# An attention and FP4 network block on one core: v's product in four column groups, row sums on GpSimd, the shift through DRAM, and a later network

## The chip, the cores and the metric

The kernel runs on one core of one Trainium2 chip. A time is device microseconds of one execution of the whole program. Three runs of the kernel before took 4761.64, 4766.83 and 4768.15 us; the median is 4766.83 us. A core has five engines with an instruction stream each: TensorE (PE, with its weight loads shown apart as PEld), VectorE (DVE), ScalarE (ACT), GpSimd (POOL) and SyncE (SP), which issues all DMAs of this program. Each engine executes its stream in order; semaphores tie the streams together.

## The reference

The input x has 8 batches of 1024 tokens with 512 features, in float32. Cut to what matters:

```python
xn = layernorm(x)                                  # no scale, no bias
q, k, v = split(xn @ W_attn + b_attn, 3)           # 16 heads of 32 features
att = softmax(where(causal, q @ k.T * 32**-0.5, -inf))
attn = (att @ v) @ W_proj + b_proj
fq = fp4_quant_dequant                             # blocks of 16: scale = max|x| / 6, round to E2M1
h = silu(fq(xn) @ fq(w_gate).T) * (fq(xn) @ fq(w_up).T)      # 1408 hidden features
out = x + attn + fq(h) @ fq(w_down).T
```

## The kernel before, in words

Tokens are worked on in 64 tiles of 128. Attention is worked on in 64 units, each two heads (HU) of one batch; a batch has eight tiles and eight units.

`prepare` takes a normalised tile, transposes it, keeps its quantised form for the network in DRAM (`keep_quantised`), and at every second tile calls `project`, which makes q, k and v for two tiles in six steps. q and k are split into a rounded part and a rest, `high` and `low`, so that the scores can be made with one-pass float32r products; they go to DRAM with v. In the kernel before v carries a 33rd column of ones per head (VW = 33), so that the product of weights and v yields the row sums too.

`maxima(un)` makes all scores of a unit once (L407), masks the diagonal blocks and takes row maxima on VectorE (L415, L417). The negated maxima, again in a rounded part and a rest, are placed in a sparse tile `shift`, transposed in four pieces (L433) and copied to `shT` by ScalarE (L435).

`weigh(un)` makes the scores a second time, keys along partitions. For each half Q of the queries and each block j of 128 keys, and for each head r, one product adds the shift (L466), another the scores (L469), ScalarE takes the exponential (L477) into a buffer `pr` (eight of them), and GpSimd clears what lies above the diagonal (L480). The products with v are delayed: `weighted()` issues those of the waiting key blocks (L449, fp32, heads at partitions 0 and 64 of one PSUM tile `y`) after the scores of a later block. In the kernel before this is called at every odd j and at the end, so the blocks hold keys 0, then 1 and 2, then 3 and 4, and so on. The result is copied by ScalarE (L498) and stored; `invert` fetches the row sums of a unit, takes reciprocals on VectorE and stores them.

`network` goes through the tiles in chunks of 512, 512 and 384 hidden features: gate and up products (L557), SiLU on ScalarE, product and quantisation on VectorE (`quantised`, ten instructions), transposes (L215), and the down product (L542). Its result plus x and the projection's bias is kept in DRAM as `part`. `finish` fetches y and the inverses of a tile, multiplies them (L625), multiplies with W_proj (L632; its two halves come again and again through a ring with one buffer), adds `part` (L637) and stores the output.

What sets the order. TensorE, ScalarE and SyncE follow the order in which the Python program emits instructions; VectorE and GpSimd are ordered by a scheduler from the dependencies. `merge` interleaves several generators ("streams"): each yields the estimated cost of what it has just emitted, and the next to go on is the one that has got least far through the total given for it. `Later(us, action)` emits an action, mostly a DMA, when the sum of all yielded costs has grown by so much. The loop over n runs, for unit n, these streams together: `begin(n + AHEAD)` (the preparation of a tile ten units ahead), `finish` of an earlier tile, `weigh(units[n])`, one tile of the network, and `maxima(units[n + 1])`. The network lags by LAG = 5 units: in units 0 to 4 the remaining pieces of the network's weights are quantised instead, and the first eight tiles are quantised (`prepare_late`). There are 34 weight pieces, of which a third is quantised ahead of the loop, in the head, where the first batch is projected. After the loop follow the last tiles of the network and the remaining calls of `finish`.

PSUM has six buffers named g that all products share in turn, one buffer y and one buffer acc.

## Time and profile before

| | value |
|---|---|
| median of three runs | 4766.83 us |
| the profiled execution: its own time / its span | 4757.63 us / 4755.9 us |
| granted clock of TensorE over the span | 0.976 of full speed |
| TensorE / VectorE / ScalarE / GpSimd busy | 4490.6 / 2794.9 / 1505.3 / 491.1 us |
| DMA | 590.38 MB, queue busy 44.7% of 16 engines |
| y (L449), 3072 records | 606.8 us busy |
| exponentials (L477), 1536 | 668.7 us busy |
| selects (L480), 1024 | 360.0 us busy |
| first / last record of L449 | 209.8 us / 4555.1 us |

How to read it. The span is that of the profiled execution, from its first to its last instruction. Busy time of a group is the time in which at least one of its instructions ran, so overlapping instructions count once; the mean is that of one. An fp32 product appears as two records with a weight load each, a float32r product as one. "Idle before" is the time in which the engine stood still ahead of the group, and the arrow names what ended the wait. In the chain of work that ended last each step is followed back to what released it.

### The profile page before, as it was taken

What the parts mean: (1) busy time and instruction counts of PE and PEld (TensorE: products, weight loads), DVE (VectorE), ACT (ScalarE), POOL (GpSimd) and SP (SyncE); (2) the same over time, 40 slices, a digit from 0 to 9 for tenths busy, and PEclk for the clock granted to TensorE, in tenths of its full rate; (3) what the DMA queues carried; (4) which work ended last, traced back from release to release, by engine and by line L of the source; (5) the groups of instructions that cost most, each with busy time, mean ns of one, the idle gap of its engine ahead of it and who ended that gap; (6) DMA issues with size and microseconds to landing.
All of it is one profiled execution on the core that took longest, in us unless ns stands there. A gap on an engine that the chain in (4) does not pass through costs nothing.

```text
span 4755.9 us, 54933 instructions
## 1 busy us (share of the span) xinstructions
PE 4490.6 (94%) x17876; PEld 2693.5 (57%) x17876; DVE 2794.9 (59%) x6841; ACT 1505.3 (32%) x2906; POOL 491.1 (10%) x1177
## 2 busy tenths in 40 slices
PE   7677899999999999999999999999999999999995
PEld 6445555555555555655555656556556555555553
DVE  6698466655556565656655656555656654566542
ACT  2133333333333333333333333333333333333310
POOL 0011111110110110110110011010111110111100
PEclk9888999999999999999999999999999999999997
DMA  6644434444453453544454454443454444333233
GB/s 208 181 138 137 111 102 109 132 128 130 114 150 106 123 135 107 139 132 117 125 146 118 121 146 118 123 128 115 128 145 122 132 123 127 98 98 94 65 91 108
DMA packets 582590, 590.38 MB, mean 124 GB/s; under 512 B 131616, under 2 KB 445984, under 8 KB 582304
## 3 DMA queue, kind: packets, MB, share of 16 engines
q1 hardware_dynamic: 582304, 586.88, 44.7%
q8 instruction: 142, 2.33, 0.2%
q14 instruction: 144, 1.18, 0.1%
HBM read 434.12 MB, written 152.57 MB: 123 GB/s over the span
## 4 chain that ended last, share of the span: by engine, by line
PE 83%; DVE 7%; DMA 6%; issue 1%; ACT 1%; SPq 1%; POOL 0%; DVEq 0%; ACTq 0%; POOLq 0%
PE g L557 24%; PE acc L542 11%; PE y L449 10%; PE g L315 8%; PE g L407 6%; PE g L466 5%; PE g L469 5%; PE g L632 5%; PE g L352 4%; PE g L215 2%; DMA inv_y<-inv_kept 2%; DVE scale L195 1%; DMA wp<-in_L_attn_W_proj_dram 1%; DMA qs<-qk_kept 1%; PE g L433 1%
## 5 line engine op out<-in xcount | busy, mean ns | idle before, releaser
L477 ACT ACTIVATE pr<-g 128x512 f32<-128x512 f32 (+3 forms) x1536 | 668.7, 492 | 1082.0 <-PE g L469 1072.8
L417 DVE TENSOR_REDUCE neg<-g 128x1 f32<-128x512 f32 (+3 forms) x1024 | 585.3, 582 | 230.0 <-PE g L407 225.7
L466 PE MATMUL g<-shT,pick 128*128 128x512 f32 (+3 forms) x1536 | 672.2, 447 | 20.3 <-DVE neg L417 16.3
L557 PE MATMUL g<-wgT,xqT_in 128*128 128x512 f32 (+1 forms) x1536 | 674.9, 566 | 13.8 <-DMA xqT_in<-xq_kept 13.4
L407 PE MATMUL g<-ks,qs 128*128 128x512 f32 (+3 forms) x1536 | 664.0, 477 | 18.5 <-DVE neg L417 11.4
L542 PE MATMUL acc<-wdT,hqT 128*128 128x512 f32 x1408 | 672.2, 599 | 1.4 <-ACT hqT L216 1.4
L480 POOL TENSOR_SCALAR_AFFINE_SELECT pr<-pr 128x128 f32<-128x128 f32 x1024 | 360.0, 366 | 3021.8 <-ACT pr L477 3005.5
L557 PE MATMUL g<-wuT,xqT_in 128*128 128x512 f32 (+1 forms) x1536 | 671.5, 562 | 0.0
L449 PE MATMUL y<-pr,vs 128*33 128x512 f32 (+3 forms) x3072 | 606.8, 497 | 2.9 <-POOL pr L480 2.7
L415 DVE TENSOR_TENSOR g<-g,mask 128x128 f32<-128x128 f32 x1024 | 289.3, 293 | 482.4 <-PE g L407 477.1
L469 PE MATMUL g<-qs,ks 128*128 128x512 f32 (+3 forms) x1536 | 516.9, 348 | 0.0
L315 PE MATMUL g<-xnT,wa 128*128 128x256 f32 x2048 | 486.9, 393 | 29.4 <-DVE scale L196 12.9
L315 PEld LDWEIGHTS g<-xnT,wa 128*128 128x128 f32 x2048 | 398.4, 198 | 108.2 <-ACT xnT L216 13.9
L407 PEld LDWEIGHTS g<-ks,qs 128*128 128x128 f32 x1536 | 280.4, 191 | 306.1 <-issue 139.8
L557 PEld LDWEIGHTS g<-wgT,xqT_in 128*128 128x128 f32 x1536 | 278.5, 191 | 237.5 <-issue 184.1
L557 PEld LDWEIGHTS g<-wuT,xqT_in 128*128 128x128 f32 x1536 | 276.0, 189 | 216.4 <-issue 167.8
L542 PEld LDWEIGHTS acc<-wdT,hqT 128*128 128x128 f32 x1408 | 255.7, 189 | 230.4 <-issue 215.0
L466 PEld LDWEIGHTS g<-shT,pick 128*128 128x128 f32 x1536 | 293.6, 191 | 154.4 <-issue 65.7
L469 PEld LDWEIGHTS g<-qs,ks 128*128 128x128 f32 x1536 | 293.8, 191 | 96.8 <-issue 64.6
L449 PEld LDWEIGHTS y<-pr,vs 128*33 128x33 f32 x3072 | 138.9, 110 | 354.5 <-issue 278.2
L572 DVE TENSOR_TENSOR hid<-hid,g 128x512 f32<-128x512 f32 (+1 forms) x192 | 122.7, 639 | 306.8 <-PE g L557 288.7
L632 PE MATMUL g<-wp,yT 128*128 128x256 f32 x1024 | 253.3, 392 | 47.5 <-DVE yT L625 27.9
(87 smaller groups left out, 4201.2 us busy)
## 6 DMA issues: line engine op xcount, KB each, us to landing
wa<-in_L_attn_W_attn_dram SPq DMA_DIRECT2D x194, 512.0 KB
wp<-in_L_attn_W_proj_dram SPq DMA_DIRECT2D x131, 512.0 KB
qs<-qk_kept SPq DMA_DIRECT2D x512, 128.0 KB
ks<-qk_kept SPq DMA_DIRECT2D x512, 128.0 KB
qk_kept<-high SPq DMA_DIRECT2D x128, 256.0 KB
qk_kept<-low SPq DMA_DIRECT2D x128, 256.0 KB
res<-in_L_attn_x_dram SPq DMA_DIRECT2D x72, 256.0 KB
v_kept<-v SPq DMA_DIRECT2D x64, 264.0 KB
```

Of the source, the lines that this page charges most:

```text
L315: nc.tensor.matmul(pq[:, j, :], lhsT=wa[:, c, j * P : (j + 1) * P], rhs=xnT[:, c, :], start=(c == 0), stop=(c == NC - 1),)
L407: nc.tensor.matmul(sc[:, :n], lhsT=un.qs[Q][:, r, i * P : (i + 1) * P], rhs=un.ks[h][:, r, :n], start=True, stop=True,)
L415: nc.vector.tensor_tensor(sc[:, n - P : n], sc[:, n - P : n], mask, ALU.add)
L417: nc.vector.tensor_reduce(dst, sc[:, :n], AX.X, ALU.max, negate=True)
L449: nc.tensor.matmul(y[r * 2 * HD : r * 2 * HD + VW, q0:], lhsT=un.vs[h][:, jj, r, :], rhs=pr[:, q0:], start=(j == 0), stop=(j == last), ski ...
L466: nc.tensor.matmul(w[:, q0:], lhsT=pick[:, Q * HU + r, :], rhs=un.shT[:, q0:], start=True, stop=False)
L469: nc.tensor.matmul(w[:, q0:], lhsT=un.ks[h][:, r, jj * P : (jj + 1) * P], rhs=un.qs[Q][:, r, q0:], start=False, stop=True,)
L477: nc.scalar.activation(pr[:, q0:], w[:, q0:], AF.Exp)
L480: nc.gpsimd.affine_select(out=pr[:, q0 : q0 + P], in_=pr[:, q0 : q0 + P], compare_op=ALU.is_ge, fill=0.0, base=0, pattern=[[1, P]], channe ...
L542: nc.tensor.matmul(tl.acc, lhsT=job.hqT[:, j, :], rhs=wdT[:, i, :], start=(i == 0), stop=(i == NI - 1))
L557: nc.tensor.matmul(job.g[:, : job.w], lhsT=job.tl.xqT[:, c, :], rhs=wT[:, c, job.i0 : job.i0 + job.w], start=(c == 0), stop=(c == NC - 1),)
L632: nc.tensor.matmul(po[:, cols], lhsT=yT[:, c, :], rhs=wp[:, c, :], start=(c == 0), stop=(c == NC - 1))
```

## The change

The change has several parts.

- v loses its column of ones. Its product is placed in four groups of 32 columns: even and odd key blocks of the two heads each have 32 partitions of `y`. The blocks now hold keys 0 and 1, 2 and 3, and so on, issued after the scores of the next even block; block 1 of Q = 0 is widened by cleared columns so that both of the first two start the accumulation at full width. `y` is stored in two halves, which `finish` adds.
- The row sums come from GpSimd: `summed` adds the exponentials of a head over all key blocks into `sum0` and `sum1`, and at the end of each Q four fp32 products with a tile of ones (128 x 32) add up the partitions into `z`, 256 columns each, in the four column groups. A new `yield 0.8` stands ahead of the last block.
- The shift's 32 rows (high and rest, two Q, two heads, four tiles) are put side by side, transposed in one piece, copied, stored in DRAM and fetched with four DMAs into one of two constant `shT` tiles.
- LAG is 8 in place of 5, DRAM buffers are 4 in place of 3, half of the weight pieces are done in the head in place of a third, and the two wide products with a spread scale in each weight piece are on GpSimd.
- `low` is written over `full`, and v is copied into a buffer of `full`'s name, in place of buffers of their own. `step` has one buffer in place of two.
- `finish` comes ten units after its tile in place of nine, fetches `part` ahead of the product, adds in two halves, and for the last units uses a resident W_proj in the buffers that the ring of W_attn no longer needs. After the loop, one `finish` stands beside each network tile.
- `up_to` carries what it ran over its budget to the next call. Stream totals: weigh 18 in place of 19, maxima 7 in place of 6.5, `begin` of an even n 4 in place of 1.

```diff
-    LAG = 5
+    LAG = 8
...
+    ones = const.tile([P, HD], F32, name="ones")
+    nc.gpsimd.memset(ones, 1.0)
...
     for k in range(2):
-        sh = const.tile([P, QG, P], F32, name=f"shift{k}")
-        nc.gpsimd.memset(sh, 0.0)
+        sh = const.tile([P, W], F32R, name=f"shT{k}")
+        nc.vector.tensor_copy(sh, zeros)
         shifts.append(sh)
-    v_out = const.tile([P, QT, HEADS // 2, VW], F32, name="v")
...
+        spreader = spreader or nc.vector
+        spreader.tensor_tensor(blocks(xs), blocks(src), spread(inv), ALU.mult)
...
+        spreader.tensor_tensor(blocks(xs), blocks(xs), spread(scale), ALU.mult)
...
-            done.append((piece, quantised(raw, piece[4], raw)))
+            done.append((piece, quantised(raw, piece[4], raw, nc.gpsimd)))
...
-                low = p1.tile([P, 2, QW], F32R, name="low")
+                low = full.bitcast(F32R)
...
+            v_out = p1.tile([P, QT, 2 * P], F32, name="full")
+            nc.scalar.copy(v_out, pv)
...
-        for i in range(QG):
-            nc.tensor.transpose(pt[:, i * P : (i + 1) * P], sh[:, i, :], ident)
-        un.shT = p2.tile([P, W], F32R, name="shT")
-        nc.scalar.copy(un.shT, pt)
-        yield 0.5
+        nc.tensor.transpose(pt[:rows, :P], stat.rearrange("p e q r i -> p (e q r i)"), ident)
+        statT = p2.tile([rows, P], F32, name="statT")
+        nc.scalar.copy(statT, pt[:rows, :P])
+        yield 0.3
+        def store():
+            un.shift = dram.tile([2, 2, HU, W], F32, name="shift_kept")
+            nc.sync.dma_start(out=un.shift.rearrange("e q r (i p) -> (e q r i) p", p=P), in_=statT)
+            Later(2.5, load)
+        def load():
+            un.shT = shifts[un.n % 2]
+            for q in range(2):
+                for r in range(HU):
+                    row = (q * HU + r) * HD
+                    nc.sync.dma_start(out=un.shT.bitcast(F32)[row : row + 2, :], in_=un.shift[:, q, r, :])
+        Later(2.0, store)
...
+            sums = [p1.tile([P, W], F32, name=f"sum{r}") for r in range(HU)]
+            def summed(group):
+                for r in range(HU):
+                    prs = [(pr, q0) for _, s, pr, q0 in group if s == r]
+                    if group[0][0] == 0:
+                        nc.gpsimd.tensor_tensor(sums[r], prs[0][0], prs[1][0], ALU.add)
+                    else:
+                        for pr, q0 in prs:
+                            nc.gpsimd.tensor_tensor(sums[r][:, q0:], sums[r][:, q0:], pr[:, q0:], ALU.add)
...
+                    row = (j % 2 * HU + r) * HD
                     nc.tensor.matmul(
-                        y[r * 2 * HD : r * 2 * HD + VW, q0:],
-                        lhsT=un.vs[h][:, jj, r, :],
+                        y[row : row + HD, q0:],
+                        lhsT=un.vs[h][:, jj, r * HD : (r + 1) * HD],
                         rhs=pr[:, q0:],
-                        start=(j == 0),
-                        stop=(j == last),
+                        start=(j < 2),
+                        stop=(j >= last - 1),
                         skip_group_check=True,
+                        tile_position=(0, row),
                     )
...
-                if j % 2 == 1 and waiting:
+                if j % 2 == 0 and waiting:
                     yield weighted()
                     waiting = []
                 waiting += fresh
-            yield weighted()
+                if j % 2 == 1:
+                    summed(waiting)
+            yield 0.8
+            spent = weighted()
+            z = ps_g.tile([P, W // 2], F32, name="g")
+            for r in range(HU):
+                for half in range(2):
+                    row = (r * 2 + half) * HD
+                    nc.tensor.matmul(
+                        z[row : row + HD, :],
+                        lhsT=ones,
+                        rhs=sums[r][:, half * W // 2 : (half + 1) * W // 2],
...
+                        tile_position=(0, row),
+                    )
+            yield spent + 0.45
...
-        EARLY = PIECES // 3
+        EARLY = PIECES // 2
...
-            if n >= NT + 1:
-                streams.append((finish(tiles[n - NT - 1]), 6.4))
-            streams.append((weigh(units[n]), 19.0))
+            if n >= LAG + 2:
+                streams.append((finish(tiles[n - LAG - 2]), 6.4))
+            streams.append((weigh(units[n]), 18.0))
...
-        left = [finish(tiles[n]) for n in range(N - NT - 1, N)]
-        for n in range(N - LAG, N):
-            count = 1 if n in (N - LAG, N - 1) else 2
-            some, left = left[:count], left[count:]
-            merge([(up_to(net, TILE), TILE), (itertools.chain(*some), 6.4 * count)])
-        next(left[0])
+        for n in range(N, N + LAG):
+            some = [finish(tiles[m]) for m in ([n - LAG - 2] if n == N else []) + [n - LAG - 1]]
+            merge([(up_to(net, TILE), TILE), (itertools.chain(*some), 6.4 * len(some))])
+        end = finish(tiles[N - 1])
+        passed(next(end))
         run(net)
-        for step in left:
-            run(step)
+        run(end)
```

## The prediction

> **What bounds the kernel now.** First the page's busy shares and its 40 slices, then the chain that ended last, then the trace in five stretches, and last the groups, the timeline and the waits around the lines that change.
>
> ```profile
> PE 4490.6 (94%) x17876; PEld 2693.5 (57%) x17876; DVE 2794.9 (59%) x6841; ACT 1505.3 (32%) x2906; POOL 491.1 (10%) x1177
> PE   7677899999999999999999999999999999999995
> PE g L557 24%; PE acc L542 11%; PE y L449 10%; PE g L315 8%; PE g L407 6%; PE g L466 5%; PE g L469 5%; PE g L632 5%; PE g L352 4%; PE g L215 2%; DMA inv_y<-inv_kept 2%; DVE scale L195 1%; DMA wp<-in_L_attn_W_proj_dram 1%; DMA qs<-qk_kept 1%; PE g L433 1%
> ```
>
> TensorE is full except in the first five slices and the last. Its work is spread over many lines, and L449, the product with v, is 10% of the chain. GpSimd has 90% free. The stretches are: head, units 0 to 4 without the network, units 5 to 53, units 54 to 63 (no projections left), tail. The columns are length, then busy time of TensorE, weight loads, VectorE, ScalarE, GpSimd, then clock, DMA share and GB/s.
>
> ```profile
> 0.00:209.80 209.80, 150.16 (x636) 122.60 (x638) 125.22 (x303) 38.38 (x80) 11.10 (x31) 0.89 0.68 204
> 209.80:514.10 304.30, 218.29 (x1003) 141.87 (x1002) 252.25 (x663) 97.07 (x210) 44.72 (x97) 0.84 0.48 132
> 514.10:3985.00 3470.90, 3409.40 (x13649) 2040.50 (x13648) 2030.12 (x4968) 1157.71 (x2220) 366.82 (x880) 0.99 0.46 125
> 3985.00:4555.20 570.20, 567.86 (x2175) 306.88 (x2176) 321.95 (x779) 198.21 (x373) 64.47 (x167) 1.00 0.34 90
> 4555.20:4755.90 200.70, 144.92 (x424) 81.61 (x424) 65.32 (x133) 13.90 (x24) 4.03 (x3) 0.88 0.35 105
> ```
>
> In the third and fourth stretches (4041 us) TensorE is idle for only 64 us: there a microsecond of TensorE work removed is a microsecond gained, 70.8 us a unit in the third (3470.9 / 49), 57.0 in the fourth. Units 0 to 4 take 61 us each without any network, with VectorE busy 83%: quantising weights and late tiles sets their pace. The tail idles 56 us.
>
> ```profile
> L449 PE MATMUL y<-pr,vs 128*33 128x512 f32 (+3 forms) x3072 | 606.8, 497 | 2.9 <-POOL pr L480 2.7
> L433 PE MATMUL g<-ident,shift 128*128 128x128 f32 x256 | 39.0, 275 | 5.4 <-DVE rstd L260 2.3 <-DVE inv L198 2.2 <-DVE shift L427 0.7
> L539 POOL TENSOR_TENSOR res<-res,bp 128x512 f32<-128x512 f32 x64 | 85.0, 1328 | 597.4 <-DMA res<-in_L_attn_x_dram 467.4 <-DVE hid L207 37.6 <-DVE hid L572 33.8
> L480 POOL TENSOR_SCALAR_AFFINE_SELECT pr<-pr 128x128 f32<-128x128 f32 x1024 | 360.0, 366 | 3021.8 <-ACT pr L477 3005.5 <-DMA res<-in_L_attn_x_dram 7.3 <-POOL pr L480 0.3
> ```
>
> The timeline at one block of four y products (8 records of 512 columns), with its neighbours:
>
> ```profile
> 2542.43 0.59 PE L632 MATMUL g<-wp,yT 128*128 128x256 f32 x2
> 2542.96 1.91 PE L449 MATMUL y<-pr,vs 128*33 128x512 f32 x8
> 2544.80 0.44 PE L215 MATMUL g<-ident,hid 128*128 128x128 f32 x2
> ```
>
> An fp32 product is two records. A 512-column record on the full array takes 0.43 us (L542 x4 is 1.72 in the chain), so eight in a row would take 3.44; here they take 1.84 (2542.96 to 2544.80), four times 0.43 plus 0.12. The two heads, in different columns of the array, run at the same time. The two L632 records take 0.53 instead of 0.43: entering and leaving the narrow form costs 0.10 + 0.12 = 0.22 us a block.
>
> ```profile
> POOL rstd L261 <- DVE rstd L260: 549.1, 58, 34.2
> POOL res L539 <- DMA res<-in_L_attn_x_dram: 467.4, 34, 43.6
> PEld y L449 <- POOL pr L480: 55.0, 165, 1.2
> ```
>
> GpSimd stands for long in its own order at rstd and res, yet TensorE waits only 55 us for it.
>
> **What the Trainium skill says.** "TensorEngine Tiling (Array Packing)", Overview and Key Properties: 32 columns or fewer allow four tiles, up to 4x, and changing the mode drains the engine; the trace shows the drain (0.22 us) and 2x for two tiles, no run yet shows four. "TensorE: Matmul & The Clock Gate", Part 3, measured 2.38x for three column tiles, so less than ideal is possible. "SBUF — State Buffer", Who interferes with whom: a GpSimd instruction that reads SBUF and a VectorE instruction with two SBUF inputs exclude each other for a whole instruction; the groups above cannot show it. "GPSIMD Engine Reference", 3.1, has 4497 ns for a 2048-column add; with the trace's 1328 for 512 that gives about 270 ns + 2.06 ns a column.
>
> **The change, part by part.**
>
> *y in four groups.* A head's widths over a unit are 1280 (Q=0) + 3328 (Q=1) = 4608 columns, 9 x 0.86 = 7.7 us a unit with both heads side by side; eight blocks (keys 0 / 1,2 / 3 and 0 / 1,2 / 3,4 / 5,6 / 7) add 1.8. 64 x 9.5 = 608, which is the 606.8 of the row. Afterwards key pairs (0,1), (2,3) and so on run together and the wider sets the time: 512 + 256 + 3 x 512 + 256 = 2560 columns, 4.3 us. The products with ones add 256 columns twice, 0.86 us, inside the last blocks. Six blocks add 1.3. That is 6.5 us: 3.0 less a unit. Bounds: if only two tiles stream at a time in pairs, (A,B) then half overlapped with (C,D), three steps in place of two: 6.5 + 1.3 + 1.3 = 9.1, 0.4 less. I take four at once, since the two streams of the trace cost each other nothing.
>
> *Shift.* Three of four transposes go (39.0 x 3/4 = 29 us), one remaining narrow one may drain (64 x 0.22 = 14): 0.25 us a unit less. In exchange the shift goes through DRAM: one store and four loads, each about 0.4 us of SP's issue, two flights of 2 to 4 us as DMA steps in the chain show. Maxima end at 4.95 / 7.0 = 71% of a unit's schedule, so some 19 us are left before the next unit's L466; hidden. Without the cover it would cost about 8 us a unit. SP gains ten DMAs a unit (two y halves for two heads, four more sums, five for the shift, one yT), 4 us of issue in 70; behind them stand loads made half a unit ahead.
>
> *Sums on GpSimd.* Per head and unit: five adds of 512, one 384, two 256, two 128, that is 5 x 1.33 + 1.06 + 1.60 + 1.07 = 10.4, both heads 21 us. With selects (16 x 0.37), clears, res and rstd it is about 30 us of 67: not a bound. But three things queue behind an add: selects (y waits for them), rstd (VectorE waits), and the product with ones waits for the last add. After the last scores of Q=0 in an even unit, TensorE's order has about 1.3 us before the product with ones; a select, an add, a select, an add after the exponential end some 2.1 us after them. The odd unit has 5 us. I take 0.6 us a unit (bounds 0 and 5), with VectorE's lock: 27 two-input or double-rate instructions a unit of 0.4 to 0.7 us, met by an add about 3 times in 10, half an add each, 5 us more on an engine that is 58% busy here.
>
> *LAG 8, weights' two wide products to GpSimd, half the weights in the head.* Eight network-free units in place of five. Weight pieces per unit fall from 4.6 to 2.1, late tiles from 1.6 to 1, at about 5 and 6.6 us of VectorE (six wide steps of 0.43 to 0.69 and four small ones); two steps of each piece left go to GpSimd. 61 - 12.5 - 4 - 3 = 42, plus 8 for lock and GpSimd waits: 50 us, times 8 = 400.
>
> *Head.* Six more pieces, two steps each on GpSimd; `low` now lies in `full`, and v too: ScalarE must wait for the previous store to land. 30 steps, about 1 us each; with the pieces +25 (bounds 5 and 60).
>
> *Finish and tail.* The part is loaded before the product, wp stays resident, one finish follows each tile instead of four serial ones of about 20 us at the end. One more add on VectorE a tile (0.69). Extra budget of the network is carried over: before, 88 of 1408 L542 records (4 tiles) are left at the end, so it ran one tile ahead over 59 units, about 0.5 us each, and this returns to the tail.
>
> **Sum** against the span of 4755.9. Head 209.8 + 25 = 235. Network-free units 400. Then 46 x (70.8 - 3.25 - 0.5 + 0.6) = 46 x 67.7 = 3112. Ten x (57.0 - 3.15) = 538. Tail: a tile is (1346 + 672) / 64 = 31.5 of L557 and L542, eight make 252; ten finishes of 253.3 / 64 = 4.0 make 40; the end 20: 312. Together 4597. The profiled execution took 4757.63, the median is 9 us over that: with 11 us over the span, 4608. I say 4605.
>
> **Rivals.**
> 1. Four tiles don't all run at once. For: three tiles gave 2.38x in the skill, and the trace has two at most. Against: two are perfect. Loses 2.6 us x 56 units, 146 at the worst, half of that as likely: 4680 to 4750. The change then doesn't do what it says.
> 2. GpSimd's order becomes the wait (the other side). Adds, selects, rstd and res stand in one order; rstd waits for VectorE, which the adds lock out, and y and the ones product wait behind. For: it already stands 549 + 467 us at rstd and res, and its free share falls from 88% to 55%. Against: TensorE pays 55 us today. It takes the whole gain when TensorE's wait for POOL grows by 160 us, 3 us a unit; at 4 a unit, 4605 + 56 x 3.4 = 4795.
> 3. The longer network-free part gives nothing: VectorE and GpSimd exclude each other, units stay at 61 us: 8 x 11 = 88 more, 4693.
>
> **Chances.** As forecast 0.60 (4540 to 4670); first rival 0.18; second 0.16, two thirds of it slower; third 0.06. Measurement tells about 0.2% (9.5 us). Faster: 0.60 + 0.17 + 0.04 + 0.06, less a little, 0.85; within 0.2%: 0.03; slower 0.12. The range 4530 to 4765 leaves out the worst of the second rival and about 0.04 below.
>
> **What will show it.** y blocks of eight records of 512 near 1.0 us, L449's successor with the ones product near 415 us busy (rival 1: near 580). TensorE's wait for POOL under 120 us (rival 2: over 215). Network-free units of 50 us. wp and inv_y gone from the chain's end. Wrong would be above all an add on GpSimd far over 1.33 us, or a shift that arrives late at L466's successor.

## The result and the profile after

The changed kernel takes 4900.53 us in the median of four runs (4897.56 to 4905.14), the kernel before beside it 4765.57 (4761.64 to 4768.15). The ratio is 1.0287, with a 95% interval from 1.0274 to 1.03: slower by 135 us. The forecast was 4605, and its range ended at 4765. The profiled execution took 4902.55 us with a span of 4900.8.

The page of the changed kernel: busy shares, TensorE's slices, the granted clock in tenths, and the chain that ended last, by line and by engine. Under it stands the chain of the kernel before by engine.

```profile
PE 4482.6 (91%) x18708; PEld 2698.6 (55%) x18708; DVE 3060.8 (62%) x6903; ACT 1444.1 (29%) x2892; POOL 1836.1 (37%) x2652
PE   6567778999999999999999999999999999999999
PEclk9778889999999999999999999999999999999999
PE g L611 23%; PE acc L596 9%; PE g L322 7%; PE y L479 5%; PE g L696 4%; PE g L497 4%; PE g L414 4%; PE g L359 4%; PE g L500 4%; DVE neg L423 3%; PE g L222 2%; DVE scale L201 1%; PE g L537 1%; DVE inv L204 1%; DVE g L422 1%
PE 68%; DVE 16%; ACT 2%; DMA 2%; issue 2%; POOL 1%; SPq 1%; ACTq 0%; DVEq 0%; POOLq 0%
```

```profile
PE 83%; DVE 7%; DMA 6%; issue 1%; ACT 1%; SPq 1%; POOL 0%; DVEq 0%; ACTq 0%; POOLq 0%
```

y has gone from 10% of the chain to 5%, the ring of W_proj and the inverses have gone from it, and TensorE is full to the last slice. But VectorE's lines L423, L204 and L422 have entered it (L201 stood in it before, as L195), VectorE's share of the chain has grown from 7% to 16%, its busy time by 266 us, and six of the first seven slices are thinner. GpSimd went from 491 to 1836 us.

The same in four stretches, cut at the first exponential of units 0, 8 and 54 (so 8 to 53 is one stretch in both kernels). Columns as in the prediction: length, then busy time of TensorE, weight loads, VectorE, ScalarE, GpSimd, then clock, DMA share, GB/s. First the changed kernel, then the second and third stretch of the kernel before.

```profile
0.00:252.00 252.00, 158.48 (x640) 128.38 (x641) 138.31 (x319) 38.58 (x81) 50.39 (x64) 0.83 0.58 176
252.00:755.80 503.80, 350.41 (x1645) 227.98 (x1645) 339.94 (x759) 140.02 (x315) 250.74 (x352) 0.84 0.43 117
755.80:4050.10 3294.30, 3150.39 (x13305) 1894.93 (x13305) 2062.14 (x4707) 1042.50 (x2069) 1256.48 (x1839) 0.97 0.47 132
4050.10:4900.80 850.70, 823.29 (x3122) 447.29 (x3120) 520.43 (x1118) 223.00 (x429) 278.48 (x397) 0.99 0.30 81
```

```profile
207.20:714.80 507.60, 421.02 (x1816) 262.71 (x1816) 373.74 (x957) 169.49 (x349) 66.43 (x148) 0.91 0.45 123
714.80:3979.90 3265.10, 3204.88 (x12829) 1919.04 (x12828) 1905.17 (x4665) 1085.11 (x2082) 343.97 (x827) 0.99 0.46 126
```

The forecast had 235, 400, 3112 and 850 (538 + 312). The head is 17 over, the network-free units 104, units 8 to 53 182. The last number was hit, but by two misses that cancel (see the points on the prediction). In the third stretch TensorE is busy 54 us less than before, and the stretch is 29 us longer: its idle time rose from 60 to 144 us, and its clock fell from 0.99 to 0.97.

The groups of the adds, of y and of the product with ones:

```profile
L472 POOL TENSOR_TENSOR sum<-sum,pr 128x512 f32<-128x512 f32 (+3 forms) x1024 | 948.4, 935 | 605.8 <-ACT pr L508 560.7
L479 PE MATMUL y<-pr,vs 128*32 128x512 f32 (+3 forms) x3072 | 431.2, 516 | 24.1 <-POOL pr L511 23.3
L537 PE MATMUL g<-sum,ones 128*32 128x256 f32 x1024 | 126.6, 391 | 0.2 <-POOL sum L472 0.2
```

And one block of y in the timeline:

```profile
2235.90 1.06 PE L479 MATMUL y<-pr,vs 128*32 128x512 f32 x8
2236.89 0.28 PE L437 MATMUL g<-ident,stat 128*32 128x128 f32 x1
```

Eight records of 512 take 0.99 us where they took 1.84 (2542.96 to 2544.80 in the prediction): four groups do run at once. The product with ones takes 126.6 / 128 = 0.99 us each instead of the 0.43 assumed.

Most of TensorE's idle time in the third stretch (103 of 144 us) lies at two lines of the changed kernel, where it waits for row maxima. Each line is the product waiting, what it waits for, the sum in us, how often, and the longest; the longest ones, of 2.1 us, come at each of the two places once in two units. The second fence has the longest wait of the kernel before in the same part of its span.

```profile
PE g L497 <- DVE neg L423: 55.3, 48, 2.1
PE g L611 <- DVE neg L423: 47.7, 23, 2.1
```

```profile
PE g L215 <- DVE xs L208: 39.6, 11, 7.8
```

One hole at L611, first TensorE, then VectorE meanwhile, then TensorE's clock in windows of 1 us:

```profile
2208.66 0.50 PE L414 MATMUL g<-ks,qs 128*128 128x512 f32 x1
2211.29 3.64 PE L611 MATMUL g<-wuT,xqT_in 128*128 128x512 f32 x4 [2.13 <-DVE neg L423]
```

```profile
2206.59 0.69 DVE L201 TENSOR_REDUCE scale<-hid 128x32 f32<-128x512 f32 x1
2207.19 0.68 DVE L201 TENSOR_REDUCE scale<-xt 128x32 f32<-128x512 f32 x1
...
2209.42 0.68 DVE L208 TENSOR_TENSOR xs<-xt,inv 128x512 f32<-128x512 f32 x1
2210.02 0.42 DVE L209 TENSOR_SCALAR step<-hid 128x512 int32<-128x512 int32 x1
2210.36 0.29 DVE L422 TENSOR_TENSOR g<-g,mask 128x128 f32<-128x128 f32 x1
2210.56 0.88 DVE L423 TENSOR_REDUCE neg<-g 128x1 f32<-128x512 f32 x2
```

```profile
2210.00:2211.00 1.00, 0.00 (x0) 0.00 (x0) 1.00 (x4) 0.00 (x0) 0.00 (x0) 1.00 0.78 227
2211.00:2212.00 1.00, 0.71 (x1) 0.36 (x2) 1.00 (x5) 0.00 (x0) 0.00 (x0) 0.74 0.14 51
2212.00:2213.00 1.00, 1.00 (x2) 0.34 (x1) 1.00 (x3) 0.00 (x0) 0.00 (x0) 0.50 0.00 0
2213.00:2214.00 1.00, 1.00 (x4) 0.46 (x2) 1.00 (x3) 0.00 (x0) 0.00 (x0) 0.50 0.00 0
2214.00:2215.00 1.00, 1.00 (x4) 0.48 (x3) 0.90 (x2) 0.00 (x0) 0.00 (x0) 0.56 0.00 0
2215.00:2216.00 1.00, 1.00 (x4) 0.49 (x4) 0.88 (x4) 0.00 (x0) 0.00 (x0) 1.00 0.00 0
```

The up product needs a score buffer g that a row maximum still holds. VectorE, busy without a gap, does two quantisings (hid and xs, interleaved) ahead of that maximum. At L497 it is the norm of the next tile, and the cast and subtraction of a projection, that stand ahead of it. TensorE stands still for 2.13 us and then works at half clock until about 2215: the four products take 3.64 us where four others took 1.72 in the chain of the prediction. The clock column puts a size on it. What is missing from 1.00 in the four windows from 2211 to 2215 is 0.26 + 0.50 + 0.50 + 0.44 = 1.7 us of full speed, that is 3.4 us at half clock. With the 2.13 us of standing this hole costs some 3.8 us.

The granted clock in the trace has only the values 0.5 and 1.0 in units 8 to 53. It shows 46 stretches of half clock in the changed kernel, 44 of them of 3.4 us, and 7 in the kernel before. Summed up they lose 83 us of full speed there, against 19 before. Of 44 holes of 2.1 us, 43 are followed by half clock.

### The profile page after: what moved, and what is told of

Its sections match the earlier page's. It is cut to its first block, busy times and chain, and to the rows that moved or that the text cites. A ratio compares the mean times of both kernels' runs of the same rounds, so it can differ in the third digit from the quotient of the medians.

```text
span 4900.8 us, 59197 instructions
## 1 busy us (share of the span) xinstructions
PE 4482.6 (91%) x18708; PEld 2698.6 (55%) x18708; DVE 3060.8 (62%) x6903; ACT 1444.1 (29%) x2892; POOL 1836.1 (37%) x2652
## 4 chain that ended last, share of the span: by engine, by line
PE 68%; DVE 16%; ACT 2%; DMA 2%; issue 2%; POOL 1%; SPq 1%; ACTq 0%; DVEq 0%; POOLq 0%
PE g L611 23%; PE acc L596 9%; PE g L322 7%; PE y L479 5%; PE g L696 4%; PE g L497 4%; PE g L414 4%; PE g L359 4%; PE g L500 4%; DVE neg L423 3%; PE g L222 2%; DVE scale L201 1%; PE g L537 1%; DVE inv L204 1%; DVE g L422 1%
## 5 line engine op out<-in xcount | busy, mean ns | idle before, releaser
L472 POOL TENSOR_TENSOR sum<-sum,pr 128x512 f32<-128x512 f32 (+3 forms) x1024 | 948.4, 935 | 605.8 <-ACT pr L508 560.7
L423 DVE TENSOR_REDUCE neg<-g 128x1 f32<-128x512 f32 (+3 forms) x1536 | 811.5, 548 | 79.3 <-PE g L414 69.1
L414 PE MATMUL g<-ks,qs 128*128 128x512 f32 (+3 forms) x1536 | 694.6, 499 | 88.6 <-ACT full L333 43.6
L611 PE MATMUL g<-wuT,xqT_in 128*128 128x512 f32 (+1 forms) x1536 | 707.8, 591 | 47.7 <-DVE neg L423 47.7
L497 PE MATMUL g<-shT,pick 128*128 128x512 f32 (+3 forms) x1536 | 646.3, 429 | 83.6 <-DVE neg L423 64.9
L611 PE MATMUL g<-wgT,xqT_in 128*128 128x512 f32 (+1 forms) x1536 | 678.9, 568 | 1.7
L422 DVE TENSOR_TENSOR g<-g,mask 128x128 f32<-128x128 f32 x1024 | 286.8, 291 | 557.8 <-PE g L414 555.0
L322 PE MATMUL g<-xnT,wa 128*128 128x256 f32 x2048 | 504.4, 403 | 42.4 <-ACT xnT L223 26.1
L469 POOL TENSOR_TENSOR sum<-pr 128x512 f32<-128x512 f32 x256 | 339.7, 1339 | 485.7 <-ACT pr L508 475.7
L322 PEld LDWEIGHTS g<-xnT,wa 128*128 128x128 f32 x2048 | 417.7, 206 | 120.1 <-ACT xnT L223 27.6
L611 PEld LDWEIGHTS g<-wuT,xqT_in 128*128 128x128 f32 x1536 | 286.5, 196 | 316.1 <-issue 201.7
L479 PE MATMUL y<-pr,vs 128*32 128x512 f32 (+3 forms) x3072 | 431.2, 516 | 24.1 <-POOL pr L511 23.3
L497 PEld LDWEIGHTS g<-shT,pick 128*128 128x128 f32 x1536 | 298.9, 195 | 244.9 <-DVE neg L423 109.1
L611 PEld LDWEIGHTS g<-wgT,xqT_in 128*128 128x128 f32 x1536 | 280.8, 191 | 234.5 <-issue 169.4
L333 ACT ACTIVATE full<-g,bqk 128x256 f32<-128x256 f32 x256 | 107.3, 470 | 626.0 <-PE g L322 307.7
```

The costliest lines, as they stand in the source:

```text
L322: nc.tensor.matmul(pq[:, j, :], lhsT=wa[:, c, j * P : (j + 1) * P], rhs=xnT[:, c, :], start=(c == 0), stop=(c == NC - 1),)
L414: nc.tensor.matmul(sc[:, :n], lhsT=un.qs[Q][:, r, i * P : (i + 1) * P], rhs=un.ks[h][:, r, :n], start=True, stop=True,)
L423: nc.vector.tensor_reduce(neg[:, Q + h, k : k + 1], sc[:, :n], AX.X, ALU.max, negate=True)
L469: nc.gpsimd.tensor_tensor(sums[r], prs[0][0], prs[1][0], ALU.add)
L472: nc.gpsimd.tensor_tensor(sums[r][:, q0:], sums[r][:, q0:], pr[:, q0:], ALU.add)
L479: nc.tensor.matmul(y[row : row + HD, q0:], lhsT=un.vs[h][:, jj, r * HD : (r + 1) * HD], rhs=pr[:, q0:], start=(j < 2), stop=(j >= last - 1 ...
```

## The experiments

All times are medians in us; beside each stand runs of the kernel before, taken together with it (medians 4759 to 4767). The four stretches are those of above. For units 8 to 53 follow TensorE's busy and idle time, and the full speed lost to half clock, summed from the clock records of the trace.

| kernel | time | ratio to before, 95% | head | units 0-7 | units 8-53 | rest | busy / idle, 8-53 | lost to half clock, 8-53 |
|---|---|---|---|---|---|---|---|---|
| before | 4765.6 | | 207 | 508 | 3265 | 776 | 3205 / 60 | 19 |
| after | 4900.5 | 1.0274-1.0300 | 252 | 504 | 3294 | 851 | 3150 / 144 | 83 |
| no_adds | 4794.2 | 1.0057-1.0087 | 249 | 450 | 3257 | 836 | 3110 / 147 | 65 |
| clears | 4903.3 | 1.0290-1.0336 | 252 | 457 | 3347 | 840 | 3090 / 257 | 123 |
| before_adds | 4937.7 | 1.0357-1.0388 | 209 | 552 | 3392 | 791 | 3254 / 138 | 58 |
| no_adds_later | 4758.5 | 0.9978-0.9992 | 246 | 454 | 3212 | 840 | 3058 / 154 | 27 |
| after_later | 4897.8 | 1.0256-1.0287 | 250 | 503 | 3287 | 851 | 3108 / 179 | 40 |
| no_adds_light | 4716.5 | 0.9888-0.9918 | 247 | 449 | 3191 | 823 | 3059 / 132 | 44 |
| after_light | 4801.3 | 1.0065-1.0095 | 249 | 503 | 3218 | 834 | 3090 / 127 | 49 |
| before_light | 4737.3 | 0.9932-0.9962 | 208 | 507 | 3248 | 773 | 3202 / 46 | 15 |
| own_buffers | 4867.6 | 1.0192-1.0222 | 232 | 492 | 3292 | 850 | 3146 / 146 | 77 |
| weights_dve | 4888.6 | 1.0241-1.0274 | 244 | 495 | 3291 | 851 | 3144 / 147 | 77 |
| sibling | 4741.5 | 0.9944-0.9973 | 235 | 407 | 3242 | 855 | 3172 / 70 | 15 |
| sibling_four | 4683.5 | 0.9816-0.9849 | 238 | 387 | 3216 | 840 | 3052 / 164 | 43 |
| sibling_dram | 4784.2 | 1.0032-1.0062 | 244 | 448 | 3237 | 853 | 3162 / 76 | 14 |
| sibling_own_dram | 4768.7 | 1.0005-1.0019 | 234 | 445 | 3240 | 854 | 3164 / 76 | 15 |
| sibling_dram_late | 4946.3 | 1.0366-1.0400 | 243 | 464 | 3370 | 867 | 3202 / 168 | 73 |
| sibling_own | 4731.8 | 0.9917-0.9951 | 227 | 410 | 3241 | 853 | 3172 / 69 | 15 |
| sibling_own_dve | 4712.6 | 0.9882-0.9911 | 222 | 397 | 3237 | 854 | 3169 / 67 | 12 |
| sibling_own_lag5 | 4820.6 | 1.0110-1.0140 | 215 | 497 | 3345 | 766 | 3205 / 140 | 29 |

### What the adds cost

**no_adds** leaves 1024 of the 1280 adds out of the changed kernel (the first of each Q stays):

```diff
-                    else:
-                        for pr, q0 in prs:
-                            nc.gpsimd.tensor_tensor(sums[r][:, q0:], sums[r][:, q0:], pr[:, q0:], ALU.add)
```

> The changed kernel with only the first of the adds on GpSimd in each Q (256 of 1280); the other 1024 are left out, so the row sums are incomplete. Lock theory (an add and VectorE's two-input instructions exclude each other, VectorE falls behind, TensorE waits for score buffers) and order theory (selects, rstd and the product with ones queue behind adds on GpSimd) both expect units of the long middle part at about 68 us in place of 71.7 and a time near 4700. Schedule theory (the adds are harmless, the new budgets, the later network and the shared buffers cost the time) expects 4860 to 4900.

106 us less, about half in units 0 to 7 (54) and 38 in units 8 to 53. The time lies between what the two sides expected: the adds are a cause, and not the only one: without them the kernel is still 32 us above the kernel before.

**clears** puts two clears of the same width in the place of every add; they write and don't read SBUF, and the row sums are left out:

```diff
-                            nc.gpsimd.tensor_tensor(sums[r][:, q0:], sums[r][:, q0:], pr[:, q0:], ALU.add)
+                            for _ in range(2):
+                                nc.gpsimd.memset(sums[r][:, q0:], 1.0)
```

> The changed kernel with every add replaced by two writes of constant ones over the same columns: GpSimd is busy nearly as long (about 1.05 us for 512 columns in place of 1.34) and in the same order, but reads nothing from SBUF; the row sums are left out. Lock theory expects VectorE's two-input instructions back at 0.69 us and a time within 40 us of the run without adds. Order theory expects a time within 40 us of the changed kernel, 4860 to 4900.

As slow as with the adds, but for another reason. VectorE is hardly stretched (1935 us busy in units 8 to 53 against 1921 without adds and 2062 with them). The clears need nothing from anyone, so GpSimd runs them in a heap and the norm's rstd stands behind it. The timeline of this kernel, at a place that comes once in two units:

```profile
2255.75 2.38 POOL L474 MEMSET sum<- 128x384 f32 x10
2258.09 0.55 POOL L268 TENSOR_TENSOR rstd<-rstd,power 128x1 f32<-128x1 f32 x1
2258.68 0.55 DVE L269 TENSOR_SCALAR xt<-xt,mv,rstd 128x512 f32<-128x512 f32 x1 [5.73 <-POOL rstd L268]
...
2261.11 0.80 PE L499 MATMUL g<-shT,pick 128*128 128x512 f32 x1 [7.17 <-DVE neg L423]
```

VectorE waits 5.73 us for rstd, the maxima stand behind it, and TensorE waits 7.17 us for a score buffer. VectorE's wait for rstd in units 8 to 53 is about 140 us here, 28.5 in the changed kernel and 28.6 without adds. TensorE never waits for GpSimd at y there with the adds, and 10.2 us without them. So in units 8 to 53 the adds don't act through GpSimd's order; this run shows what rival 2 of the prediction looks like when it does happen. Units 0 to 7 are another matter: there TensorE waits 23.3 us for GpSimd at y, 14.1 without the adds, and adds and selects are some 7% of the changed kernel's chain, so that a part of the 54 us may lie in GpSimd's order. The clears wait for nothing and don't repeat the order of the adds, so they can't tell.

**before_adds** gives the kernel before one add of its own width after each block of weights, with `step` in one buffer to make room; nothing reads the sum:

```diff
+                    nc.gpsimd.tensor_tensor(sums[:, q0:], pr[:, q0:], pr[:, q0:], ALU.add)
```

> The kernel before with one add of 128 to 512 columns on GpSimd for every block of exponentials, into a scratch buffer that nothing reads (step has one buffer to make room); nothing else changes. Lock and order theories expect it slower by 150 to 300 us, 4920 to 5070, with VectorE's two-input instructions longer by 0.1 to 0.4 us. Schedule theory expects at most 40 us more than before.

176 us slower than the kernel before, for 1362 us of adds (1536 of them): 0.13 us for each microsecond of add. In the changed kernel it was 106 for 948, 0.11. VectorE's busy time in units 8 to 53 grows from 1905 to 2067 us. The adds stretch VectorE here too. `step` has one buffer in this kernel, which was not tried apart, so a part of the 176 us may belong to that.

The groups of VectorE in the changed kernel by shape show where, and under them the same steps in the kernel before:

```profile
L208 DVE TENSOR_TENSOR hid<-hid,inv 128x512 f32<-128x512 f32 x128 | 102.6, 802 | 1.7
L213 DVE TENSOR_TENSOR xs<-xs,step 128x512 f32<-128x512 f32 x56 | 62.7, 1120 | 0.4
L430 DVE CAST neg_high<-neg 128x16 fp32r<-128x16 f32 x64 | 46.6, 728 | 1.1
```

```profile
L201 DVE TENSOR_TENSOR hid<-hid,inv 128x512 f32<-128x512 f32 x158 | 108.2, 685 | 3.7 <-PE g L315 0.5
L206 DVE TENSOR_TENSOR xs<-xs,step 128x512 f32<-128x512 f32 x56 | 38.3, 684 | 0.7
L421 DVE CAST neg_high<-neg 128x16 fp32r<-128x16 f32 x64 | 10.7, 168 | 1.5
```

Without the 1024 adds the first takes 686 ns and the cast 174 in the median. The second still takes 1091 (L214 in `no_adds`), so the 256 first adds, or something else, stretch it. The maxima, which read PSUM, keep their 682 ns. For the steps with two inputs that agrees with the Trainium skill, "SBUF — State Buffer", Who interferes with whom, by which a VectorE instruction with two SBUF inputs contends with a GpSimd instruction that reads SBUF. The cast has one input and waits as well.

### The middle: VectorE's order and the clock

**no_adds_later** and **after_later** emit the norm of the next tile 8 us of the planner's clock later, without the adds and with them:

```diff
-            normed(tiles[tl.n + 1])
+            following = tiles[tl.n + 1]
+            if tl.n < NT + 2:
+                normed(following)
+            else:
+                following.ready = Later(8.0, lambda: normed(following))
```

> The kernel without the adds (1024 of the 1280 adds on GpSimd left out, so the output has wrong row sums), with one more edit: in units the norm of the next tile, its quantising included (some 15 VectorE instructions), is emitted 8 us of the planner's clock later. Theory (a pile-up on VectorE, then the clock): the profile without adds shows TensorE idle 2.7 us ahead of the product with the up weights once in two units, and 2.1 us ahead of a score once in two units, both while VectorE works off a norm or a quantising ahead of a maximum, and the granted clock at 0.50 for about 3.4 us after each. Moved by 8 us the norm falls in a stretch where VectorE is free: both waits go, the mean clock of units 8 to 53 rises from 0.98 to over 0.99, and the time falls from 4794 to 4640-4700. Rival (VectorE's total work or the finish's waits bound the middle, the place doesn't matter): 4770 to 4810, the idle turns up elsewhere.

> The changed kernel, complete, with the norm of the next tile emitted 8 us later as in the kernel without adds. Theory: the two fixed waits and the half clock after them go here too, 4900 becomes 4770 to 4830; what is left above the kernel without adds is the stretched VectorE, some 100 us. Rival (the adds' lock on VectorE makes the waits, wherever the norm stands): 4880 to 4920.

Both theories were half right, and without adds the time lies between their ranges. Without adds the clock over the span rose from 0.964 to 0.971 (some 35 us of full speed) and the time fell by 36 to 40 us: the half clock costs what it loses. But TensorE's idle time did not fall (147 to 154 us): the hole of 2.1 us ahead of a score stayed, and the other became a wait of 1.9 us ahead of a maximum. With adds the clock rose as much (0.957 to 0.965), but VectorE's busy time grew by 60 us in units 8 to 53, TensorE's idle time by 35, and nothing was gained. The place of one job decides here how much half clock follows, while the waiting stays.

**no_adds_light, after_light, before_light** leave two of the ten quantising steps out for the network's hidden features, which are then not rounded:

```diff
-        nc.vector.tensor_tensor(xs, xs, step, ALU.add)
-        nc.vector.tensor_tensor(xs, xs, step, ALU.subtract)
+        if rounded:
+            nc.vector.tensor_tensor(xs, xs, step, ALU.add)
+            nc.vector.tensor_tensor(xs, xs, step, ALU.subtract)
```

> The kernel without the adds, and of the network's quantising the two VectorE steps that add and subtract the rounding step are left out too (six instructions of 0.69 us a unit, some 4.1 us of VectorE's 42; the output is not rounded there, beside having wrong row sums). TensorE's work is unchanged. Theory (in the stretches where scores are reduced VectorE is the bound, and the 3 us a unit that y gives back are spent waiting for it): the waits of TensorE for the maxima and the half clock after them shrink, units 8 to 53 go from 70.8 to 68 or 69 us each, 4794 becomes 4660 to 4720. Rival (TensorE's own order, DMA or the finish set the pace of the middle): 4770 or more.

> The changed kernel with its adds, and the same two steps of the network's quantising left out (its output is not rounded there). They take about 1.1 us each here, so VectorE is relieved of 6.6 us a unit. Theory: 4900 becomes 4750 to 4800, more than without the adds, since VectorE is the bound for longer. Rival (GpSimd's order holds y up): over 4870.

> The kernel before with the same two steps left out (its output is not rounded there). TensorE is the bound of its middle, so the same relief of 4.1 us a unit gives little: some of its 40 us of waits for quantised tokens and of the idle ends between matmuls, 4762 becomes 4715 to 4755. If it falls as far as the kernel without adds does (by 80 us or more), VectorE was a bound of the kernel before as well.

TensorE's work is the same in all three. In units 8 to 53 the relief gives the kernel before 17 us, the one without adds 66, the changed one 77; over the whole 24, 78 and 99. So a microsecond on VectorE is three to four and a half times as dear after the change as before. It is not the waits for the maxima that shrink: those at L609 and L495, the two places of above, are 60.9 and 55.4 us in `no_adds_light`, 47.8 and 57.6 in `after_light`, and TensorE's idle time falls by only 15 and 17 us. About 21 of the 66 and 34 of the 77 us are half clock that no longer follows; the rest lies in time that the profile counts as busy. Net of the clock the three gains are about 13, 45 and 43 us, still over three times as much after the change. These runs show that the changed kernel has become sensitive to VectorE's work, not that the holes come from the amount of it. `after_light` ended just above its range: its expectation priced the two steps with those of the tokens (1.1 us each), while those left out take 0.7, and the relief was 150 / 46 = 3.3 us of VectorE a unit, not 6.6. Without adds a unit takes 69.4 us where 68 to 69 stood.

### The parts alone

**sibling** is the changed kernel with y in two groups and the ones in v as before, no adds, the shift on chip; eight network-free units, two weight steps on GpSimd, `low` in `full`, finish and tail stay as changed, while the totals of the streams `weigh` and `maxima` are as before:

```diff
-    ones = const.tile([P, HD], F32, name="ones")
...
-                            nc.gpsimd.tensor_tensor(sums[r][:, q0:], sums[r][:, q0:], pr[:, q0:], ALU.add)
...
-                        tile_position=(0, row),
...
-        Later(2.0, store)
+        for i in range(QG):
+            nc.tensor.transpose(pt[:, i * P : (i + 1) * P], sh[:, i, :], ident)
```

> The changed kernel with three parts undone: v with its column of ones in two column groups, no adds on GpSimd, the shift transposed on chip in four pieces. The later network, the weights' steps on GpSimd, low inside full, finish and tail stay. Lock and order theories expect it faster than before, 4660 to 4720, since tail and finish gain and nothing is added beside them. Schedule theory expects 4850 or more.

Those edits together are worth 20 us (0.3 to 0.6%), less than either theory that blames the adds expected, and far from the third. Units 0 to 7 take 51 us each. That is not the forecast's 50 come true: 8 of the 50 were for adds and waits that this form doesn't have.

**sibling_four** puts y in four groups on it, with the order that this needs: the blocks come after the scores of even key blocks and hold keys 0 and 1, 2 and 3, and so on, and the planner counts them half as dear, with `weigh`'s total kept. Left out are the row sums (ones are stored) and the second partial sum of y:

```diff
-                        y[r * 2 * HD : r * 2 * HD + VW, q0:],
-                        lhsT=un.vs[h][:, jj, r, :],
+                        y[(j % 2 * HU + r) * HD : (j % 2 * HU + r + 1) * HD, q0:],
+                        lhsT=un.vs[h][:, jj, r, :HD],
```

> The form with y in two groups and the shift on chip (4741.5 us), with y in four column groups alone. Left out: the row sums (ones are stored in their place) and the second partial sum of y, so the output is wrong; there are no adds and no product with ones. TensorE does some 3.9 us less a unit. If y's gain becomes time where nothing else comes with it: 4741 - 56 x 3.9 = 4523, up to 4580. If VectorE's order takes it: half or less of it shows, 4640 or more, with TensorE's waits for a maximum and the time at half clock grown beside it.

It gains 58 us of 218. y's own busy time falls from 607.3 to 408.2 us. The stretch of units 8 to 53 and the longest wait in it, first of `sibling`, then of this kernel:

```profile
642.40:3884.20 3241.80, 3172.09 (x12706) 1901.44 (x12705) 1870.87 (x4663) 1067.50 (x2069) 332.93 (x826) 1.00 0.46 126
PE g L472 <- DVE neg L423: 44.8, 45, 2.0
```

```profile
625.50:3841.90 3216.40, 3051.98 (x12707) 1886.12 (x12706) 1932.50 (x4663) 1016.53 (x1978) 357.21 (x918) 0.99 0.46 127
PE g L415 <- DVE more L425: 91.7, 44, 3.6
```

TensorE is busy 120 us less there, in spite of 27 us more of half clock; so some 147 us of full-speed work are gone, 3.2 us a unit where 218 / 56 = 3.9 were expected. Of these 95 come back as idle time, 27 as half clock, and 25 are gained. The waits for maxima grow from 46 to 128 us, with no add, no product with ones, no trip through DRAM and no second part in the kernel: holes of 3.6 us come once in two units, with VectorE busy without a gap and two quantisings ahead of the maximum. Whether VectorE lacks the time, or only has its work in the wrong place for the new order, these runs don't separate: those that do little but move work in the order (`no_adds_later`, `sibling_dram_late`, `sibling_own_lag5`) move units 8 to 53 by 45 to 133 us.

**sibling_dram** puts the shift through DRAM alone on it, as the changed kernel has it; **sibling_own_dram** gives `low` its own buffer beside that, and **sibling_dram_late** emits the store 8 in place of 2 us after the maxima:

```diff
-        Later(2.0, store)
+        Later(8.0, store)
```

> The form with y in two groups (4741.5 us), complete, with the shift through one transpose and DRAM in place of four transposes on chip, as in the changed kernel. The forecast had 0.25 us a unit less, 4728, hidden behind 19 us of slack. Rival (it comes late where units are short and the queue is full, in units 0 to 7, and its load's wait stands ahead of the scores): 4760 to 4785, units 0 to 7 at 430 to 450 us in place of 407.

> The form with y in two groups and own buffers for the low halves in the first eight projections (4731.8 us), complete, with the shift through DRAM (4784.2 without the own buffers). If ScalarE's wait for the store of the low half, held up in SyncE's order, carries the cost: 4735 to 4750, units 0 to 7 at 410 to 425 us. If it is the trip of the shift: 4770 to 4780.

> The form with the shift through DRAM (4784.2 us), complete, with the store of statT emitted 8 us of the planner's clock after the maxima in place of 2. If SyncE standing behind statT carries the cost: 4750 to 4765. If the trip itself is what is late: it gets longer by up to 6 us in each of the first eight units, 4800 to 4840. In later units 19 us of slack cover it.

The trip costs 43 us, 8 in the head and 40 in units 0 to 7, less some in units 8 to 53, where it is hidden as the prediction said (3237 us with it, 3242 without). ScalarE's wait for `low` is not the way: own buffers give 15 us back by the medians (10 without the trip), nearly all in the head. SyncE's standing doesn't show as the cause either: with the later store its 46 us of waits for statT in units 0 to 7 are gone, and the kernel is slower by 162 us, far over both expected ranges, 133 of them in units 8 to 53. But the late store doesn't show that the slack there is less than six microseconds. The shift's loads are issued some 20 us ahead of their use, and of TensorE's 168 us of idle time only 20 are waits for the shift; 110 are waits for maxima, in holes of 4.4 us once in two units:

```profile
PE g L485 <- DVE neg L424: 110.1, 43, 4.4
PE g L485 <- DMA shT<-shift_kept: 20.2, 22, 2.0
```

What moved VectorE's work ahead of the maxima there is open. In units 0 to 7 TensorE's direct waits for the shift, here in `sibling_own_dram`, are less than half of the 40; where the rest arises stays open too:

```profile
PE g L489 <- DMA shT<-shift_kept: 18.5, 6, 5.3
```

### Buffers, weights and the lag

**own_buffers** gives `low` and v buffers of their own in the first ten projections of the changed kernel (lent by the buffers that `finish` needs later), **sibling_own** `low` in the first eight of `sibling`; **weights_dve** and **sibling_own_dve** put all steps of the weights back on VectorE:

```diff
-                low = full.bitcast(F32R)
+                low = p1.tile([P, 2, QW], F32R, name="yT1") if own else full.bitcast(F32R)
...
-            v_out = p1.tile([P, QT, 2 * P], F32, name="full")
+            v_out = p1.tile([P, QT, 2 * P], F32, name="yT0" if own else "full")
```

```diff
-            done.append((piece, quantised(raw, piece[4], raw, nc.gpsimd)))
+            done.append((piece, quantised(raw, piece[4], raw)))
```

> The changed kernel, complete, but in the first 10 projections (the head and the first units) the low halves of q and k and the values of v lie in buffers of their own and no longer in the one that the projection's output is written to. Theory (ScalarE waits for the store of the low half, 12 to 13 us at the longest, and TensorE behind it): the head falls from 252 to 225-235 us, units 0 to 7 from 504 to 480-490, the time from 4900 to 4855-4875. Rival (VectorE and GpSimd set the pace of the head and of these units, the store is hidden behind them): within 10 us of 4900.

> Complete: y in two groups with the column of ones in v, the shift on chip, the other edits of the change kept (eight network-free units, two steps of the weights on GpSimd, finish and tail); new is that the low halves of q and k have a buffer of their own in the first eight projections. It ran in 4741.5 without that. If the store of the low half holds ScalarE up in the head as it did in the changed kernel (33 us with v's as well): 4705 to 4730. If it was v's store that did: within 8 us of 4741.

> The changed kernel, complete, with all six steps of the weights' quantising on VectorE again, as before the change. If moving two of them to GpSimd paid (VectorE was 83% busy in units 0 to 4 before): head and units 0 to 7 get longer by 40 us and more, 4930 to 4960. If GpSimd's multiplications (mean over 1 us, with VectorE locked out meanwhile) cost as much as they took off: within 15 us of 4900. If they cost more: under 4880, with units 0 to 7 under 480 us.

> The form with y in two groups and own buffers for the low halves (4731.8 us), complete, with all six steps of the weights' quantising on VectorE. There are no adds here for VectorE to be locked out by. If GpSimd's two steps relieve VectorE there: 4745 to 4765, head and units 0 to 7 longer. If they cost as much as in the changed kernel (12 us lost): 4715 to 4725.

The shared buffer costs 33 us in the changed kernel, 20 of them in the head, as expected (units 0 to 7 came to 491.5 us where 480 to 490 stood), and 10 in the form without v in it. The steps on GpSimd don't pay in either form: taking them back gains 12 us in the changed kernel, at the edge of the noise, and a clear 19 in `sibling_own`. `sibling_own_dve`, at 4712.55 us (0.9 to 1.2% under the kernel before), is the fastest complete version of this study.

**sibling_own_lag5** goes back to five network-free units, a third of the weights in the head, and two finishes to a tile at the end:

```diff
-    LAG = 8
+    LAG = 5
...
-        EARLY = PIECES // 2
+        EARLY = PIECES // 3
```

> The same form (4731.8 us), complete, with the network five tiles behind, a third of the weights in the head and the last finishes two to a tile, as far as the kernel before has it. If eight network-free units only move work from the first stretches to the tail: within 12 us of 4732. If their lighter VectorE is worth something: 4750 to 4780, the first units at 60 us each. If the longer tail is the worse: 4700 to 4720.

89 us slower, more than any of the three readings expected. Units 0 to 7 (now with three network tiles) are 87 longer and the rest 88 shorter, as if work had only moved. The loss is 104 us in units 8 to 53, which hold the same work in both: TensorE's idle time there is 140 instead of 69 us; the longest of its waits there are of shift transposes for VectorE (56.9 us). So how the network's chunks fall against the units seems to decide that much; which fall is the bad one was not tried.

## Why the prediction was wrong, point by point

- **"There a microsecond of TensorE work removed is a microsecond gained."** This step failed, and the forecast of units 8 to 53, 182 us too low, rests on it. TensorE's work did fall: the changed kernel is busy 54 us less there and has 83 - 19 = 64 us more of half clock, so up to 118 us of full-speed work are gone, 2.6 us a unit where 3.25 + 0.5 stood; the stretch is 29 us longer. In `no_adds` TensorE is busy 95 us less than before, and idle 86 us more. In `sibling_four`, with y alone changed, some 147 us of work gone are 25 us gained, 95 idle and 27 half clock. TensorE's 98% said that it was nearly never idle at its former pace. It did not say how much slack VectorE had behind the six score buffers: once the products with v are shorter, TensorE asks for a buffer while VectorE, at 100% in those stretches, still has two quantisings or a norm ahead of the maximum that holds it. Whether VectorE's time or the place of its work is short was not separated. The adds' own part there, 38 us for the 28 forecast, explains only 10 of the 182. The forecast should have looked at VectorE in windows of a few us, not at its 58% for the stretch.
- **The clock** was no term of the sum. The profiled span lost (1 - 0.957) x 4900.8 = 211 us of full speed, against 114 before. In units 8 to 53 it is 83 against 19; half clock follows the holes ahead of L611 and L497.
- **y in four groups: 3.0 us a unit.** The mechanism was right, the four run at once, and rival 1 is out: eight records of 512 take 0.99 us. y without the ones was to lose 9.5 - 5.6 = 3.9 us a unit; `sibling_four` shows 3.2. It is busy 431 us (408 in `sibling_four`) where 64 x 5.6 = 358 stood; part of the first is half clock, the rest was not taken apart. The product with ones was mis-sized: 0.99 us each (two a unit) for 0.43. So the two rows are busy 557.8 us, near the 580 named as rival 1's sign, for another reason.
- **GpSimd's adds: 0.6 us a unit, and 8 in a network-free one.** The estimated prices held for the wide ones (1339 to 1355, 1009 and 738 ns for 512, 384 and 256 columns, 466 for 128 where 535 stood). The lock was right in kind: VectorE's busy time grew by 141 / 46 = 3.1 us a unit where 5 stood. The adds cost 38 / 46 = 0.8 us a unit in units 8 to 53, and 54 / 8 = 6.7 in units 0 to 7.
- **"50 us" a network-free unit.** 63 measured. Of the sum 42 + 8 the second term held (6.7); the first failed, and the trip of the shift was no part of it. Without adds and trip a unit takes 51 (`sibling`) or 50 (`sibling_own_dve`) instead of 42; the trip adds 5. 51 + 6.7 + 5 is the 63. "-3" for two steps moved to GpSimd had the wrong sign; which part of "-12.5" for fewer weight pieces was too much was not tried apart.
- **The shift: hidden behind 19 us of slack.** It is hidden in units 8 to 53. It is not in the head and in the network-free units, for which the prediction made no allowance: 8 and 40 us, 43 in all.
- **Head +25.** Measured +45, inside the bounds of 5 and 60; the shared buffer is 20 of it.
- **Finish and tail: 850.** Held to a microsecond, by luck. The last record of L479 lies at 4615.8: units 54 to 63 took 566 us where 538 stood, and the tail 285 where 312 stood. Those units had taken 575 before, so they gained about 1 us each, not 3.15: here too little of the work removed was gained.
- **Rivals.** The second, on the slower side, had the right side and a wrong path. TensorE's waits for GpSimd, most of them of its weight loads, are 105.0 + 23.3 us for the selects ahead of y and about 50 for the sums, 179 in all, a growth of about 118: less than the 160 it asked for, and between the two signs (under 120, over 215). TensorE itself stands idle for GpSimd at y and at the ones for 23.5 us only, and GpSimd's order is not what holds in units 8 to 53 (`clears` shows what that would be). The third, that the longer network-free part gives nothing, came true for the changed kernel: eight units take 504 us where 508 stood, for work that had fallen.

Added up from the parts, with their effects taken as independent: -20 (the other edits), -58 (y), +43 (the trip), +106 (the adds) make 71 of the 135 us. The other 64 lie between `sibling_four` with the trip and `no_adds`: the product with ones in a score buffer, v in the shared buffer, 256 first adds, the second part of y in the finish, the totals of the streams and the new `yield 0.8`. An estimate from two forms gives 23 of them to v's buffer (33 less 10); the rest was not taken apart.

## What to carry to other kernels

A busy share near 100% tells which engine is late now, not how far the next one is behind; before pricing work off the bound, count what the second engine must do ahead of the buffers that the first waits for, in windows as short as those buffers last. A hole in TensorE's stream costs its length and, where half clock follows, here about 1.7 us more; whether it follows was not a matter of the length alone, so read it from the clock of the trace. An add on GpSimd is paid on VectorE: count the two-input instructions and the casts that it will meet, where VectorE is full, not on average.

## What the runs showed that was not expected

- A hole of 2.13 us was followed by half clock for about 3.4 us. The Trainium skill, "TensorE: Matmul & The Clock Gate", Part 1, names an idle window of about 3.4 us; the return after about 3.4 us of work agrees, the length of the hole does not. Nor does any one length decide: of the holes of 2.1 us in units 8 to 53, 43 of 44 are followed by half clock in the changed kernel, 24 of 44 in `after_light` and 1 of 22 in `no_adds_later`. What decides is open.
- GpSimd's adds stretch even a cast of 16 columns with one input (L430), from 168 to 728 ns; without the 1024 adds it takes 174.
- Ten clears run in 2.38 us, hardly stretch VectorE, and still cost as much as the adds, through a 0.55 us instruction of one column behind them.
- Eight records with the ones, in four groups of 256 columns, take 0.99 us in the changed kernel and 105.3 / 128 = 0.82 without adds, nearly as long as eight of 512 with v. Why they don't take half of that was not tried.
